# The last group's end on VectorE and ScalarE instead of accumulating transfers, and a reordered handover between two layers

## The chip, the cores and the metric

The kernel runs on one core of a Trainium2 chip. A core has TensorE (matrix products into PSUM), VectorE, ScalarE and GpSimd (elementwise work), and SyncE, whose queue issues most of the DMA transfers; ScalarE and GpSimd can issue transfers too. In the profile they are called PE, DVE, ACT, POOL and SP; SPq, ACTq and POOLq are their instruction queues. The metric is the time of one execution on the device in microseconds (us), and lower is better.

## What is computed

Two layers of attention over a graph of 4096 nodes with 512 features, all in float32. `adj` is a 4096 x 4096 matrix of edge weights, mostly zero.

```python
# layer 0
h = maximum(layernorm(x), 0)
q, k, v = h @ Wq.T + bq, h @ Wk.T + bk, h @ Wv.T + bv
x = x + softmax(q @ k.T / sqrt(512) + adj + adj) @ v
# layer 1: 8 heads of 64 features
h = maximum(layernorm(x), 0)
nX = a_ln * (X - mean) / (std + 1e-6) + b_ln        # X = h @ W, per head
kg = leaky_relu(nX @ a1 + (nX @ a2).T, 0.2) * adj    # per head, 4096 x 4096
y = softmax(where(adj != 0, kg, -32768)) @ nX + nX
out = x + elu(y)
```

The last two lines matter here. To the weighted sum of a head its own rows `nX` are added, then comes ELU, which is `maximum(y, 0) + exp(minimum(y, 0)) - 1`, and then the residual `x`, the output of layer 0.

## The kernel before

**Layer 0.** The queries are worked off in 8 chunks of 512 (`ic`), and within a chunk the keys in 32 blocks of 128 (`jt`). At the end of a chunk `chunk_end` multiplies the sums by the inverse totals and adds the rows of `x` (L810, L815), then `rows_done` updates two guards `low0` and `high0` (L824, L825). For all chunks but the last, `make_ready` spreads the work of turning the finished 512 rows into features for layer 1 over the next chunk. The features go to DRAM (`nX_d`), the own rows (`own_d`) and the rows of `x` after layer 0 (`x1_d`) too, and so do the small vectors that the scores of layer 1 are made of (`z1_d`, `z2_d`, `u4_d`, `at2m`). For the last chunk there is no next chunk; its `make_ready` runs with `last=True` inside the first steps of layer 1.

**Layer 1.** It has 512 steps, numbered n: 8 chunks of 512 queries (`ic`), 2 groups of 4 heads (`hg`), 32 blocks of 128 keys (`jt`). A step has these parts, each issued for its own n:

- `z_sums` (TensorE, L970 and L978): linear scores and masks are summed in PSUM tiles `d`. The small factors are `z1` of the group and `z2`, the masks `nb` and `nx`. The tag `d` has three buffers, and the small tiles `m` of `make_ready` and `pt1` of a group's end are taken from the same three.
- `relu` (ScalarE, L986): the upper part of the leaky ReLU for two of the four heads.
- `leaky` (VectorE, L996, L1001, L1002): the leaky ReLU for the other two heads with the broadcast rows `u4` (in the profile `u`), the product with the edge weights `g` for one head (in some steps two), and a sum for the first two.
- `weigh` (GpSimd, L1009): the product with `g` for the other three heads (or two).
- `exponent` (ScalarE, L1012), three steps later, and `values` (TensorE, L1025), four steps later, which sums into `acc`.

The edge weights and masks of four steps are loaded at a time by `load_adj` (L915 `z2`, L919 `nb`, L925 twice `nx`, L930 `g`), all on SP's queue. `open_group` loads `z1` (L943) and the two broadcasts `u4` (L946) of a group of 32 steps, ten steps ahead on SP's queue; only the first group's is called on ScalarE's queue, ahead of `load_adj(0)` in the program. `load_features` (L1109) brings the 8 blocks of features into SBUF during the first 32 steps.

**The order of the work.** Instructions marked with `seq` keep the order in which the program records them on their engine. A few others, such as the guards at the very end (L1173 to L1191), are placed by a scheduler between them. In `make_ready` a call of `at_step(d, f)` puts `f` into step 1 + d of layer 1 ahead of `leaky`; with `late=True` it comes behind `weigh`, `z_sums` and `relu` of that step. With `last=True` the statistics of the last rows, `stats` (four pairs L180 and L181 on VectorE), are called at once and thus come ahead of step 0. `deviations` (eight small operations on GpSimd, L266 to L270) and the first `norm` (ScalarE, L276) are in step 1. The transfers on SP's queue are issued in order, and each also waits for the transfer recorded eight transfers before it.

**The end of a group.** When the last `values` of a group are issued, `finish` spreads its end over the next steps, in the dictionary `later`: copies out of PSUM on ScalarE (`copies`, L1041), turning them into rows on TensorE (`to_rows`, L1047), the division (`divide`, L1056 and L1057 on VectorE), and then

- the own rows are added to `y` by an accumulating transfer that GpSimd issues (`add`, L1063),
- `minus` (L1072) and `exps` (L1076) on ScalarE make exp(minimum(y, 0)) in `e`, `positive` (L1079) makes maximum(y, 0), and `less_one` (L1082) subtracts 1,
- two more accumulating transfers (L1063) add `y` and the rows of `x1_d` to `e`,
- `close` (L1087) stores the two halves of `e` from SP's queue.

For 15 of the 16 groups this lies beside the steps of the next group. After the last group there is nothing beside it. Then the guards are reduced to one flag, which every engine loads (L73) before the kernel ends; with the given data the general path behind the flag is not entered.

Of the kernel before, what the change touches and what calls it, by code (L numbers as in the profile page):

```python
# [10 lines left out]
F32 = mybir.dt.float32  # L11
BF16 = mybir.dt.bfloat16
AF = mybir.ActivationFunctionType
ALU = mybir.AluOpType
# [4 lines left out]
P = 128  # L19
# [16 lines left out]
GC = 512  # L36
NI = N // GC
HG = 4
# [40 lines left out]
def fast_path(  # L79
# [18 lines left out]
    nc = tc.nc  # L98
    seq = tc.keep_in_program_order
# [42 lines left out]
    x1_d = dram.tile([NI, 2, P, 2, SB, P], F32, name="x1_d")  # L142
# [10 lines left out]
    own_d = dram.tile([NI, 2, P, 2, SB, P], F32, name="own_d")  # L153
# [21 lines left out]
    def means(pool, rows, name):  # L175

        st = pool.tile([P, SB, 6], F32, name=f"{name}st", tag=f"{name}st", bufs=2)
        mv = pool.tile([P, SB, 2], F32, name=f"{name}mv", tag=f"{name}mv", bufs=2)
        for b in range(SB):
            seq(nc.vector.bn_stats(st[:, b, :], rows[b]))  # L180
            seq(nc.vector.bn_aggr(mv[:, b, :], st[:, b, :]))  # L181
        return mv
# [65 lines left out]
    def make_ready(ic, x1s, small, at_step, gap, last):  # L248

        n = SB * NH  # L250
# [9 lines left out]
        def stats():  # L260
            state["mv"] = means(prep, x1s, "l")
# [164 lines left out]
            nc.sync.dma_start(out=u4_d[rows].rearrange("b h p -> (b h) p"), in_=u4c)  # L426

        if last:
            stats()
        else:  # L430
            at_step(0, stats)
        at_step(0 if last else 1, deviations)
        for b in range(SB):
            d = (0 if last else 2) + gap * b
# [28 lines left out]
    def store_rows(ic, x1s):  # L463
        for b in range(SB):
            store_block(nc.sync, x1_d, ic, b, x1s[b])


    with tc.tile_pool(name="early", bufs=2) as early, tc.tile_pool(name="kv", bufs=1) as kv:
# [70 lines left out]
        with tc.tile_pool(name="proj_c", bufs=1) as pc, tc.tile_pool(  # L539
            name="proj", bufs=2  # L540
# [96 lines left out]
            def room(first, blocks, m):  # L637
                return v[:, first : first + blocks, :].rearrange(
                    "p b d -> p (b d)"
                ).rearrange("p (m c) -> p m c", m=m)  # L640
# [37 lines left out]
            for sb in range(1, NS):  # L678
# [4 lines left out]
                if sb == 1:  # L683
                    seq(nc.sync.dma_start(
                        out=w1_sb.rearrange("p k h e -> p k (h e)"),
                        in_=w1.rearrange("(k p) o -> p k o", p=P),
# [16 lines left out]
        with tc.tile_pool(name="attn", bufs=2) as work, tc.tile_pool(  # L703
            name="attn_ps", bufs=2, space=PSUM
# [142 lines left out]
            for s in range(0, n_tiles, 2):  # L847
                ic, jt = TILES[s]
# [48 lines left out]
    with tc.tile_pool(name="ga_in", bufs=2) as inputs, tc.tile_pool(  # L897
        name="ga_g", bufs=2
    ) as adjs, tc.tile_pool(name="gat", bufs=1) as gat, tc.tile_pool(
        name="ga", bufs=2  # L900
# [3 lines left out]
        n_steps = len(STEPS)  # L904
# [30 lines left out]
        def cols(ic, hg):  # L935
            rows = slice(ic * GC, (ic + 1) * GC)
            return rows, slice(hg * HG * HD, (hg + 1) * HG * HD)

        def open_group(n, queue):

            ic, hg, _ = STEPS[n]
            z1 = inputs.tile([P, GC], BF16, name="z1", tag="z1", bufs=2)
            seq(queue.dma_start(out=z1, in_=z1_d[:, hg, ts(ic, GC)]))  # L943
            u4 = inputs.tile([P, 2, GC], F32, name="u4", tag="u4", bufs=2)
            for e in range(2):
                seq(queue.dma_start(  # L946
                    out=u4[:, e, :].rearrange("p (b i) -> p b i", i=P),
                    in_=u4_d[ic * SB : (ic + 1) * SB, hg * HG + 2 + e, :]
                    .unsqueeze(0).to_broadcast([P, SB, P]),
                ))  # L950
            groups[ic, hg] = {"z1": z1, "u4": u4}

        def pair_rows(ap, ic, hg):

            r, c = cols(ic, hg)
            return [
                ap[r, c.start + f * P : c.start + (f + 1) * P].rearrange("(b p) d -> p b d", p=P)
                for f in range(2)
            ]
# [70 lines left out]
        def finish(n, ic, hg):  # L1030

            grp = groups.pop((ic, hg))
            ob = work.tile([P, 2, GC], F32, name="ob", tag="ob", bufs=1)
            y = work.tile([P, 2, SB * 2, HD], F32, name="y", tag="y", bufs=1)

            def room():
                grp["e"] = work.tile([P, 2, SB * 2, HD], F32, name="e", tag="ob", bufs=1)

            def copies():
                for hf in range(2):  # L1040
                    seq(nc.scalar.copy(ob[:, hf, :], grp["acc"][hf]))  # L1041

            def to_rows(hf):
                pt = psum.tile([P, 2, GC], F32, name="pt1", tag="d", bufs=3)
                for b in range(SB):
                    col = (b % 2) * 2 * HB
                    seq(nc.tensor.matmul(  # L1047
                        pt[:, b // 2, col : col + 2 * HB], ob[:, hf, ts(b, P)],
                        back.rearrange("p e c -> p (e c)"), start=True, stop=True,
                    ))  # L1050
                grp["pt"] = pt[:, :, 0 : 4 * HB].rearrange("p k (q c) -> p k q c", c=HB)

            def divide(hf):
                v = grp.pop("pt")
                rinv = inverses[:, ic, hg, hf]
                seq(nc.vector.reciprocal(rinv, v[:, :, :, HD]))  # L1056
                seq(nc.vector.tensor_mul(  # L1057
                    y[:, hf].rearrange("p (k q) e -> p k q e", k=2), v[:, :, :, 0:HD],
                    rinv.unsqueeze(3).to_broadcast([P, 2, 4, HD]),
                ))  # L1060

            def add(t, what):
                seq(nc.gpsimd.dma_start(out=flat(t), in_=what, accum_op=ALU.add))  # L1063

            def of_group(ap):
                return ap[ic, hg].rearrange("p f b d -> p (f b d)")

            def flat(t):
                return t.rearrange("p f q e -> p (f q e)")

            def minus(hf):
                seq(nc.scalar.activation(grp["e"][:, hf], y[:, hf], AF.Relu, scale=-1.0))  # L1072

            def exps(hf):
                e = grp["e"][:, hf]
                seq(nc.scalar.activation(e, e, AF.Exp, scale=-1.0))  # L1076

            def positive():
                seq(nc.scalar.activation(flat(y), flat(y), AF.Relu))  # L1079

            def less_one():
                seq(nc.scalar.add(flat(grp["e"]), flat(grp["e"]), -1.0))  # L1082

            def close():
                e = grp["e"]
                for f, ap in enumerate(pair_rows(out, ic, hg)):
                    nc.sync.dma_start(  # L1087
                        out=ap, in_=e[:, f].rearrange("p (b h) e -> p b (h e)", h=2)
                    )

            for d, place, f in (
                (0, "mid", copies),
                (1, "mid", lambda: to_rows(0)), (1, "end", lambda: divide(0)),
                (2, "mid", lambda: to_rows(1)), (2, "end", lambda: divide(1)),
                (3, "end", lambda: add(y, of_group(own_d))),
                (6, "end", room), (6, "end", lambda: minus(0)), (7, "end", lambda: minus(1)),
                (8, "end", lambda: exps(0)), (8, "end", positive), (9, "end", lambda: exps(1)),
                (10, "end", less_one), (11, "end", lambda: add(grp["e"], flat(y))),
                (14, "end", lambda: add(grp["e"], of_group(x1_d))), (17, "end", close),
            ):  # L1100
                later.setdefault((n + d, place), []).append(f)

        open_group(0, nc.scalar)
        load_adj(0)

        def load_features(k):
# [15 lines left out]
        def at_step(d, f, *a, late=False):  # L1122
            (left_late if late else left).setdefault(1 + d, []).append(lambda: f(*a))
# [9 lines left out]
            for f in later.pop((n, place), []):  # L1133
                f()

        for n in range(n_steps + 22):

            q = n // JB + 1
            if n == 1:
                store_rows(NI - 1, last_rows)  # L1140
            if n % JB == (2 if q == NS - 1 else 0) and q < n_steps // JB:
                load_adj(q)
                if q < NS:
                    load_features(q)
            if n + 10 < n_steps and STEPS[n + 10][2] == 0:
                open_group(n + 10, nc.sync)
            extra(n, "top")
            if 0 <= n - 4 < n_steps:
                values(n - 4)
                if n % JB == 3:  # L1150
                    loads.pop((n - 4) // JB)
                if STEPS[n - 4][2] == NB - 1:
                    finish(n, *STEPS[n - 4][:2])
            if 0 <= n - 3 < n_steps:
                exponent(n - 3)
            extra(n, "mid")
            for f in left.pop(n, []):
                f()
            if n % JB == 2 and n // JB < NS:
                ones_in(n // JB)  # L1160
            if n < n_steps:
                leaky(n)
                weigh(n)
            if n + 1 < n_steps:
                z_sums(n + 1)
                relu(n + 1)
            for f in left_late.pop(n, []):
                f()
            extra(n, "end")
# [425 lines left out]
```

## Time and profile before

| | |
|---|---|
| time of the runs | 3947.59 us median of 3, from 3941.22 to 3955.6 |
| the profiled execution | 3945.4 us, its span 3943.6 us |
| mean TensorE clock granted | 0.987 |
| TensorE busy (PE) | 3697.2 us, 94% |
| VectorE busy (DVE) | 2869.3 us, 73% |
| GpSimd busy (POOL) | 2501.3 us, 63% |
| ScalarE busy (ACT) | 1779.9 us, 45% |

Busy shares are means over two layers with different limits. Layer 0 ends at about 2097 us; from 2400 to 2800 us, within layer 1, GpSimd is busy for 396.88 of 400 us, VectorE for 378.59, TensorE for 366.21 and ScalarE for 343.36. A line of the timeline reads: start in us from the span's start, duration in us, engine, line of the kernel, operation, output and inputs by the program's names, shapes, and in brackets how long the engine was idle before it and what ended that. Buffer numbers and trailing digits are left out of names, so `u4` stands as `u`, `x1_d` as `x_d`. For a transfer the line is its issue; when it has landed is told separately, counted from the issue.

### The profile page before, as it was taken

The numbers are of one execution on the slowest core, as the hardware profiler recorded it, in microseconds if no ns is written. First come the engines' busy times: TensorE is split into PE (matmuls) and PEld (weight loads), VectorE is DVE, ScalarE is ACT, GpSimd is POOL, SyncE is SP. The second block draws the span as 40 slices with busy tenths as digits, with TensorE's granted clock in tenths as the row PEclk, the third lists the DMA queues.
The fourth block names the chain that finished last, engine by engine and source line by source line (L and its number), as shares of the span: only waits on it lengthen the run. The fifth ranks groups of instructions, "written<-read, shape, count | busy, mean of one in ns | idle before, by whom it ended". The sixth has DMA issues, their size and how long they took to land. (4 is left out here: it accounts for less than half of the span.)

```text
span 3943.6 us, 48614 instructions
## 1 busy us (share of the span) xinstructions
PE 3697.2 (94%) x17418; PEld 1722.2 (44%) x17418; DVE 2869.3 (73%) x4299; ACT 1779.9 (45%) x1581; POOL 2501.3 (63%) x1321
## 2 busy tenths in 40 slices
PE   8989999999999999999997889999999999999996
PEld 4446666666666666666663222222222222222221
DVE  5435556565465656556566799999999999999996
ACT  1001011111111111111114688888888888888886
POOL 3432225243252524324256899999999999999996
PEclk9999999999999999999998899999999999999998
DMA  6466766768585676767567777676676777766774
GB/s 206 178 200 192 207 179 198 210 183 225 164 216 173 199 207 190 216 176 214 164 176 190 188 188 190 184 186 183 191 191 188 189 188 196 188 185 182 189 192 107
DMA packets 622778, 746.17 MB, mean 189 GB/s; under 512 B 84672, under 2 KB 467904, under 8 KB 603072
## 3 DMA queue, kind: packets, MB, share of 16 engines
q1 hardware_dynamic: 613552, 716.05, 64.3%
q0 software_dynamic: 6912, 25.17, 3.6%
q8 instruction: 138, 2.26, 0.2%
q10 hardware_dynamic: 2064, 1.77, 0.2%
q14 instruction: 112, 0.92, 0.1%
HBM read 562.23 MB, written 172.23 MB: 186 GB/s over the span
## 5 line engine op out<-in xcount | busy, mean ns | idle before, releaser
L1009 POOL TENSOR_TENSOR t<-t,g 128x1536 f32<-128x1536 f32 (+1 forms) x512 | 1704.8, 3531 | 55.7 <-DVE t L1002 48.1
L1025 PE MATMUL acc<-t,nX 128*64 128x512 f32 x4096 | 1001.7, 610 | 49.4 <-ACT t L1012 44.3
L758 POOL TENSOR_TENSOR total<-total,aT 128x512 f32<-128x512 f32 x248 | 340.1, 1371 | 1064.0 <-ACT aT L753 1055.2
L1012 ACT ACTIVATE t<-t 128x2048 f32<-128x2048 f32 x512 | 974.9, 1905 | 1.5 <-POOL t L1009 1.5
L768 PE MATMUL acc<-v,aT 128*128 128x512 f32 x2048 | 963.0, 593 | 0.0
L753 ACT ACTIVATE aT<-aT 128x512 f32<-128x512 f32 x256 | 161.2, 630 | 1323.7 <-DVE aT L748 1301.6
L986 ACT ACTIVATE t<-d 128x1024 f32<-128x1024 f32 x512 | 524.5, 1024 | 285.0 <-PE d L978 284.8
L1002 DVE TENSOR_TENSOR t<-t,d 128x1024 f32<-128x1024 f32 x512 | 619.2, 1209 | 2.8 <-ACT t L986 2.8
L768 PEld LDWEIGHTS acc<-v,aT 128*128 128x128 f32 x2048 | 390.0, 190 | 273.7 <-issue 245.6
L1025 PEld LDWEIGHTS acc<-t,nX 128*64 128x64 f32 x4096 | 251.5, 137 | 564.5 <-issue 344.7
L970 PE MATMUL d<-z,z 6*128 6x512 bf16 x2048 | 370.9, 387 | 108.2 <-DVE t L1001 59.4
L996 DVE SCALAR_TENSOR_TENSOR d<-u,at2m,d 128x512 f32<-128x512 f32 x576 | 431.7, 749 | 39.2 <-PE d L978 34.9
L748 DVE TENSOR_TENSOR aT<-aT,X 128x256 f32<-128x256 f32 x512 | 214.6, 419 | 290.0 <-PE X L740 287.0
L1001 DVE TENSOR_TENSOR t<-d,g 128x512 f32<-128x512 f32 (+1 forms) x512 | 383.9, 750 | 14.4 <-DMA g<-gT_d 7.8
L748 DVE TENSOR_TENSOR aT<-aT,Z 128x256 f32<-128x256 f32 x384 | 159.4, 415 | 306.5 <-PE Z L740 301.8
L996 DVE SCALAR_TENSOR_TENSOR t<-u,at2m,d 128x512 f32<-128x512 f32 x448 | 334.5, 747 | 46.5 <-DVE d L996 1.4
L970 PEld LDWEIGHTS <-z 6*128 6x128 bf16 x2048 | 91.9, 91 | 624.5 <-issue 404.3
L978 PE MATMUL d<-nx,ident_b 64*64 64x512 bf16 x2048 | 321.2, 392 | 1.4 <-DMA nx<-nT_d 1.2
L978 PE MATMUL d<-nb,ident_b 64*64 64x512 bf16 x2048 | 320.7, 392 | 0.0
L732 DVE SCALAR_TENSOR_TENSOR gs<-ng,aT 128x512 f32<-128x512 bf16 x256 | 279.4, 1091 | 10.2 <-DMA gT_d<-gs 1.5
L740 PE MATMUL Z<-qt,hS 128*128 128x256 f32 x1024 | 265.7, 382 | 8.3 <-DVE aT L748 8.3
L740 PE MATMUL X<-qt,hT 128*128 128x256 f32 x1024 | 264.3, 381 | 0.5 <-DVE aT L748 0.5
(171 smaller groups left out, 3154.2 us busy)
## 6 DMA issues: line engine op xcount, KB each, us to landing
g<-gT_d SPq DMA_DIRECT2D x128, 1024.0 KB, 5.5
ag<-in_adj_dram SPq DMA_DIRECT2D x256, 256.0 KB, 5.7
hT<-h_d SPq DMA_DIRECT2D x64, 1024.0 KB, 6.0
hS<-s_d SPq DMA_DIRECT2D x64, 1024.0 KB, 8.2
gT_d<-gs SPq DMA_DIRECT2D x256, 256.0 KB, 2.8
nb<-nT_d SPq DMA_DIRECT2D x128, 512.0 KB, 4.7
nx<-nT_d SPq DMA_DIRECT2D x256, 256.0 KB, 5.6
nT_d<-ng SPq DMA_DIRECT2D x256, 128.0 KB, 3.2
```

Of the source, the lines that this page charges most:

```text
L740: seq(nc.tensor.matmul(out, a, b, start=start and k == 0, stop=k == 1, skip_group_check=not start,))
L748: seq(nc.vector.tensor_add(p, p, part))
L768: seq(nc.tensor.matmul(sums[ic][b], probs[s][:, ts(b, P)], v[:, jt, :], start=jt == 0, stop=jt == NB - 1))
L970: seq(nc.tensor.matmul(pair[hh // 2][:, hh % 2, :], z2[rows, ts(jt % JB, P)], groups[ic, hg]["z1"][rows, :], start=True, stop=False,))
L978: seq(nc.tensor.matmul(pair[hh // 2][ts(c, HD), hh % 2, :], ident_b[rows, rows], masks[r != c][rows, jt % JB, :], start=False, stop=True,))
L986: seq(nc.scalar.activation(t[:, 0:2, :], zs[n][0], AF.Relu, scale=4.0))
L996: seq(nc.vector.scalar_tensor_tensor(pair[1][:, e, :] if e > 1 - mine else t[:, 2, :], u4[:, e, :], at2m[:, jt, h : h + 1], pair[1][:, e, ...
L1001: seq(nc.vector.tensor_mul(t[:, HG - mine : HG, :], pair[1][:, 2 - mine : 2, :], g))
L1002: seq(nc.vector.tensor_add(t[:, 0:2, :], t[:, 0:2, :], pair[0]))
L1009: seq(nc.gpsimd.tensor_mul(t[:, 0:mine, :], t[:, 0:mine, :], g))
L1012: seq(nc.scalar.activation(logits[n], logits[n], AF.Exp))
L1025: seq(nc.tensor.matmul(grp["acc"][hf][ts(e, HD), :], nX[jt // SB][:, jt % SB, hg * HG + 2 * hf + e, :], t[:, 2 * hf + e, :], start=jt == 0 ...
```

## The change

It has three parts.

1. In layer 1's first steps the statistics of the last rows are no longer recorded ahead of step 0. They are put at the end of step 0, behind its `leaky` and `weigh` and behind `z_sums` and `relu` of step 1.
2. The first group's `z1` and `u4` are issued on SP's queue. As `open_group(0)` stands ahead of `load_adj(0)`, they now come first in that queue.
3. The last group's end is a straight sequence of its own. Own rows and rows of `x1_d` are loaded by two ordinary transfers into a tile of the tag `t` when the last step has been recorded. The additions are VectorE operations on halves of 128 x 512; ScalarE makes exp(minimum(y, 0)) as before; the maximum, and the sum with the -1 in it, are VectorE's. The two halves are stored from SP's and from ScalarE's queue. The loop is shortened to match.

```diff
         if last:
-            stats()
+            at_step(-1, stats, late=True)
         else:
             at_step(0, stats)
...
+            if n > n_steps:
+
+                of_rows = [last_in[0][:, 2 * k : 2 * k + 2, :] for k in range(2)]
+
+                def half(t, hf):
+                    return t[:, hf].rearrange("p q e -> p (q e)")
+
+                copies()
+                to_rows(0)
+                divide(0)
+                to_rows(1)
+                divide(1)
+                room()
+                e = grp["e"]
+                for hf in range(2):
+                    seq(nc.vector.tensor_add(half(y, hf), half(y, hf), of_rows[0][:, hf]))
+                    minus(hf)
+                    exps(hf)
+                    seq(nc.vector.tensor_scalar_max(half(y, hf), half(y, hf), 0.0))
+                for hf, queue in enumerate((nc.sync, nc.scalar)):
+                    seq(nc.vector.scalar_tensor_tensor(
+                        half(e, hf), half(e, hf), -1.0, half(y, hf), ALU.add, ALU.add
+                    ))
+                    seq(nc.vector.tensor_add(half(e, hf), half(e, hf), of_rows[1][:, hf]))
+                    queue.dma_start(
+                        out=pair_rows(out, ic, hg)[hf],
+                        in_=e[:, hf].rearrange("p (b h) e -> p b (h e)", h=2),
+                    )
+                return
...
-        open_group(0, nc.scalar)
+        open_group(0, nc.sync)
         load_adj(0)
...
-        for n in range(n_steps + 22):
+        last_in = []
+        for n in range(n_steps + 4):
 
             q = n // JB + 1
+            if n == n_steps:
+
+                last_in.append(work.tile([P, HG, GC], F32, name="t", tag="t", bufs=6))
+                for k, ap in enumerate((own_d, x1_d)):
+                    seq(nc.sync.dma_start(
+                        out=last_in[0][:, 2 * k : 2 * k + 2, :].rearrange("p f c -> p (f c)"),
+                        in_=ap[NI - 1, 1].rearrange("p f b d -> p (f b d)"),
+                    ))
```

## The prediction

> **What bounds the kernel now.** I read the page first, then the chain of waits, then the timeline of the two places that the diff touches. The page:
>
> ```profile
> span 3943.6 us, 48614 instructions
> PE 3697.2 (94%) x17418; PEld 1722.2 (44%) x17418; DVE 2869.3 (73%) x4299; ACT 1779.9 (45%) x1581; POOL 2501.3 (63%) x1321
> L1009 POOL TENSOR_TENSOR t<-t,g 128x1536 f32<-128x1536 f32 (+1 forms) x512 | 1704.8, 3531 | 55.7 <-DVE t L1002 48.1
> ```
>
> Layer 0 (to 2097 us) is TensorE's. In layer 1 VectorE and GpSimd feed each other, 95% and 99% busy (378.6 and 396.9 of 400 us from 2400): a step's `weigh` costs GpSimd 3.5 us. The change leaves TensorE's instructions in the same order, and GpSimd's too but for three accumulating DMAs at the end, so the 1800 us between the two places have no reason to change. What counts is when layer 1 starts and what lies behind its last step. There the chain of waits (start, duration, what) consists of time in which the engine waited for nothing but a transfer:
>
> ```profile
> 3908.66 7.17 issue
> 3915.96 10.40 issue
> 3927.25 4.24 issue
> ```
>
> The end, in the timeline (start, duration, engine, line; in brackets the idle time and its releaser):
>
> ```profile
> 3910.65 1.94 PE L1025 MATMUL acc<-t,nX 128*64 128x512 f32 x8 [0.59 <-ACT t L1012]
> 3914.85 0.69 DVE L1057 TENSOR_TENSOR y<-pt,inverses 128x512 f32<-128x512 f32 x1
> 3915.84 0.89 POOL L1063 DMA_DIRECT2D y<-own_d  x1 [7.19 <-DVE y L1057]
> 3921.86 1.15 ACT L1072 ACTIVATE e<-y 128x512 f32<-128x512 f32 x2 [8.63 <-DMA y<-own_d]
> 3925.02 1.06 ACT L1082 ACTIVATE e<-e 128x1024 f32<-128x1024 f32 x1
> 3926.38 0.87 POOL L1063 DMA_DIRECT2D e<-y  x1 [9.64 <-ACT e L1082]
> 3931.50 0.87 POOL L1063 DMA_DIRECT2D e<-x_d  x1 [4.25 <-DMA e<-y]
> 3936.98 0.93 SPq L1087 DMA_DIRECT2D out_dram<-e  x2
> ```
>
> After the last division (ends 3915.54) every stage waits for a transfer: own rows 6.0 us from issue, ELU on ScalarE 4.2, then two more additions by DMA, 5.1 and 5.5 us from start to the next start. 21.4 us in a row, nothing beside it.
>
> The handover, also in the timeline:
>
> ```profile
> 2085.53 0.33 SPq L915 DMA_DIRECT2D z<-z_d  x1
> 2086.66 1.18 ACTq L946 DMA_DIRECT2D u<-u_d  x2
> 2087.72 0.60 SPq L930 DMA_DIRECT2D g<-gT_d  x1
> 2098.44 1.02 ACT L986 ACTIVATE t<-d 128x1024 f32<-128x1024 f32 x1 [11.76 <-PE d L978]
> 2100.20 0.18 DVE L181 BATCH_NORM_AGGREGATE lmv<-lst 128x2 f32<-128x6 f32 x1
> 2102.27 0.75 DVE L996 SCALAR_TENSOR_TENSOR d<-u,at2m,d 128x512 f32<-128x512 f32 x1 [1.89 <-DMA u<-u_d]
> 2105.67 3.45 POOL L1009 TENSOR_TENSOR t<-t,g 128x1536 f32<-128x1536 f32 x1 [17.59 <-DVE t L1002]
> 2114.07 1.22 DVE L1002 TENSOR_TENSOR t<-t,d 128x1024 f32<-128x1024 f32 x1 [2.80 <-ACT t L986]
> ```
>
> VectorE does the last rows' statistics (2097.10 to 2100.38), then waits 1.89 us for the broadcasts `u4`. The landing answers say 15.0 us for the second broadcast (2087.1 to 2102.1) and 14.0 us for `g`:
>
> ```profile
> DMA to landing us min/median/max: 9.5/12.2/15.0
> DMA to landing us min/median/max: 14.0/14.0/14.0
> ```
>
> `g` lands at 2087.7 + 14.0 = 2101.7, only 0.4 us before `u4`. It is wanted next (L1001 at 2103.7).
>
> **What the skill says.** The Trainium skill, "DMA: Bandwidth & Descriptors", section "Queues, rings and completion order": each DMA engine consumes one queue's descriptors in ring order and takes turns between queues by packets. The trace agrees: later on, with broadcasts ahead on SP's queue, the `nb` load issued at 2334.7 lands after 10.6 us, against 3.9 us for that of 2318.3 without them. The same page, "Anatomy of one DMA — SWDGE (gpsimd) path", gives 2.0 us plus bytes over 436 GB/s, an estimate of 3.2 us for 512 KB; here the accumulating ones take 4.8 to 5.9, so I use the trace. "VectorE: DVE Perf Modes", section "Walkthrough: the 8-slice pipeline in each mode": a float32 tensor_scalar out of SBUF can run two elements per cycle, a tensor_tensor only one; L730 (0.42) and L1001 (0.68 us) agree.
>
> **The end, step by step.** The start is the same, 3915.54. Removed: three accumulating DMAs with their 6.0 + 5.1 + 5.5 us, the two whole-tile passes on ScalarE. Added on VectorE per half of 128x512: two additions (0.68 each, as L1001; an SBUF-only one was not seen, between 0.55, 512 elements at one per cycle, and 0.7), one maximum (0.42 as L730; 0.3 to 0.7), one scalar_tensor_tensor (0.75, as L996). That is 2 x 2.53 = 5.06. The flag's instructions (0.41, 0.41, 0.14, 0.14, 0.28, 0.15, 0.14) are interleaved with them by the built order, 1.6 us. ScalarE: 0.58 + 0.61 per half. In order: first addition to 3916.2; two reductions and a small one to 3917.05; ScalarE's negative part is done by 3916.85, so the maximum goes at once, to 3917.45; second addition 3918.15; ScalarE 3918.25 to 3918.85 and exp to 3919.45; VectorE waits for TensorE's small transpose until 3918.7, worst 3919.0, maximum 3919.4, then 0.75 + 0.15 + 0.68: first half at 3921.0; flag at 3921.9; second half at 3922.55. The last issue starts near 3922.65 on ScalarE's queue, against 3937.45 (the second of the two at 3936.98): 14.8 us earlier. Behind it the kernel takes about the same (here 5.7 us from the end of the issue to the end of the span: landing 2.3, flag load and branch). As the first half goes out 1.6 us earlier on SP, nothing is added there; for five engines branching together I allow 0.3. **End: 14.5 us**, from 13 to 15.5.
>
> What hides the two new loads (512 KB each, on SP at step 512): their `t` slot is free when the values of step 506 are done, near 3900.2; a 1 MB `g` takes 5.5 us (median), so they are there near 3907, 8 us before the first addition. Nothing is queued behind them but the output. Without that cover, the addition would wait as long as they are late.
>
> **The handover.** SP issues `z1` and both broadcasts first, from 2085.5: 0.34 + 1.18 = 1.5 us, and z2, `nb`, `nx`, `g` each go out 1.5 us later. ScalarE loses three issues; it idles there anyway (11.76 us). The broadcasts, now first in an idle queue at 2085.9 and 2086.5, land after 6.9 to 11.5 us (30 on SP's queue), by 2098.0 at the latest. Then the masks decide: `d` is ready for VectorE at 2098.3 now. What is late next is `g`. The bytes before it are the same 2.8 MB, so if the engines only swap the order it lands where it did, 2101.7. In the steady case above it landed 10.6 us after the second broadcast (2342.1 to 2352.7); 2094.0 + 10.6 gives 2104.6. I take 2103. The first two VectorE operations are then done, and the first step ends at 2103.0 + 0.15 + 0.6 + 1.21 = 2105.0 against 2105.54: 0.5 us won; at the ends `g` by 2099.8 wins 3.9, `g` at 2106.5 loses 3.
>
> The statistics (3.28 us) now stand between steps 0 and 1. Queued behind them is step 1 on VectorE, and `weigh(1)` for it. But GpSimd first does `weigh(0)` (3.45) and the deviations (3.08), and VectorE idles 2.80 in step 2, waiting for ScalarE behind the `norm` that waits for these deviations. Statistics end 3.3 us after step 0, GpSimd wants them 3.55 after it: covered, with 0.25 to spare. Step 1 ends 6.75 after step 0, where `weigh(1)` started 6.7 after it. Cost 0.2; if the cover fails, 0.5 (3.28 - 2.80). **Handover: +0.3**, from -3 to +3.9. Later the step rhythm is unchanged, so this shift reaches the end.
>
> **Sum.** 14.5 + 0.3 = 14.8. Of the profiled execution (3945.4 us, span 3943.6): 3930.6. The median 3947.59 is 2.2 higher: 3932.8. I say 3932, 0.4% less.
>
> **Rivals.**
> 1. The broadcasts no longer matter and `g` comes early: step 0 starts at 2098.3, ends at 2101.6, 3.9 won, 3928. For it: transfer engines were only half busy from 2090 to 2093. Against: the same half-busy stretch follows broadcasts at 2336 to 2338.
> 2. The masks and `g` queue up behind the broadcasts more than counted: `g` at 2106 to 2107, handover 2 to 3 us lost, 3935. For it: 10.6 against 3.9 us for `nb`.
> 3. Slower: the broadcasts, alone at the head of SP's queue, hold up everything behind them. Its place is `g`'s landing. If they took until 2102.1 as now and the rest only then its 10.6 us, `g` lands at 2112.7 and 10 us go: no change. The gain of the end is eaten from a landing of about 2118; with broadcasts of twice 15.0 us it is 2127, and the time 3956. Against it: 11.5 us is the longest of the 30 on SP's queue, with 1.5 MB ahead.
> 4. The end doesn't shrink fully: own rows land late, or the closing 5.7 us grow, since all engines now load the flag at once behind an output in flight. 6 us less gain, 3938. Against: engines that load the flag early took 0.5 to 1.6 us.
>
> **Numbers.** The forecast 0.64, first rival 0.12, second 0.14, third 0.04, fourth 0.06. A measurement of this kernel tells 0.3% (11.8 us) from no change; three runs of before spread over 14 us, so a median is uncertain by some 5. The likeliest case alone spans 3925 to 3940 with that; with rivals 1, 2 and half of 4, 3922 to 3943. Faster by over 0.3%: nearly all of rival 1, most of the forecast (a gain of 14.8 minus noise), a third of 2: 0.72. Slower 0.05, same 0.23.
>
> **What would show it.** In the changed profile: no GpSimd DMA at the end; last output issue 7 us after the last division (was 22); from there 5 to 6 us to the end. At the handover: L996 starts at about 2098.3 without waiting for `u4`, and L1001 waits for `g` to about 2103; `weigh(0)` near 2105; statistics behind it. Wrong if `weigh(0)` starts after 2107, if step 2 ends more than 10.5 us after step 0, or if the first addition waits for its rows.

## The result

The changed kernel takes 3937.22 us (median of 19 runs, 3930.75 to 3942.38); the kernel before, run beside it, 3943.81 (19 runs, 3938.52 to 3955.6). The ratio is 0.9983, 95% interval 0.9976 to 0.9989: 6.7 us faster (4.3 to 9.5). That is clear of zero, but within the 0.3% that were to count as no change. The forecast was 3932, a gain of 14.8. Its time is within the range; its gain is more than twice the measured one.

The page of the kernel after:

```profile
span 3931.9 us, 48617 instructions
PE 3693.1 (94%) x17418; PEld 1719.4 (44%) x17418; DVE 2873.8 (73%) x4307; ACT 1778.2 (45%) x1579; POOL 2498.0 (64%) x1318
```

Busy shares are as before, so the two places have to be read in the timeline. First the end:

```profile
3916.88 0.69 DVE L1057 TENSOR_TENSOR y<-pt,inverses 128x512 f32<-128x512 f32 x1
3917.49 0.68 DVE L1106 TENSOR_TENSOR y<-y,t 128x512 f32<-128x512 f32 x1
3918.94 0.43 DVE L1109 TENSOR_SCALAR y<-y 128x512 f32<-128x512 f32 x1
3922.49 0.39 SPq L1115 DMA_DIRECT2D out_dram<-e  x1
3923.06 0.69 DVE L1114 TENSOR_TENSOR e<-e,t 128x512 f32<-128x512 f32 x1
3923.83 0.41 ACTq L1115 DMA_DIRECT2D out_dram<-e  x1
```

No transfer stands in the chain any more: the first addition (L1106) follows the division at once, and the last issue starts 6.26 us after the last division ends (3917.57), against 21.91 before.

The handover, where the surprise is:

```profile
2083.52 0.98 SPq L946 DMA_DIRECT2D u<-u_d  x2
2085.58 3.17 SPq L925 DMA_DIRECT2D nx<-nT_d  x2
2088.79 1.02 SPq L930 DMA_DIRECT2D g<-gT_d  x1
2090.88 2.88 SPq L1138 DMA_DIRECT2D nX<-nX_d  x4
2099.72 0.76 DVE L996 SCALAR_TENSOR_TENSOR d<-u,at2m,d 128x512 f32<-128x512 f32 x1 [4.48 <-PE d L978]
2106.13 0.69 DVE L1001 TENSOR_TENSOR t<-d,g 128x512 f32<-128x512 f32 x1 [4.87 <-DMA g<-gT_d]
2108.08 3.43 POOL L1009 TENSOR_TENSOR t<-t,g 128x1536 f32<-128x1536 f32 x1 [22.37 <-DMA nX<-nX_d]
2128.73 0.69 DVE L309 COPY x<-m 128x512 f32<-128x512 f32 x1 [6.79 <-DMA x_d<-x]
```

VectorE doesn't wait for `u4` any more, but waits 4.87 us for `g`. And a second wait has appeared, 6.79 us behind stores of `x1_d`. (The bracket of L1009 names features, which landed at the same moment. `weigh(0)` starts 0.13 us after the end of L1002, as it did before.)

```profile
DMA to landing us min/median/max: 17.3/17.3/17.3
```

This is `g` from its issue at 2088.8: 17.3 us, where it was 14.0. It lands at 2106.1. It was also issued late, 5.6 us after the first transfer of the handover (L943) and not 2.2 us after it (L915) as before: the two issues of `nx` ahead of it took 3.17 us, 2.49 of them the second. Before, the two took 1.30:

```profile
2086.37 1.30 SPq L925 DMA_DIRECT2D nx<-nT_d  x2
```

The end of layer 0 moves by some microseconds from execution to execution, so the table counts from the start of the last product group of layer 0 (L806). "Step 0" is the start of the sum L1002 in step 0, "step 4" the same in step 4; "rest" is the time from the last division to the end of the span. Besides the first profiles it has a second one of before, after, and the handover alone. All in us.

| kernel | L806 at | step 0 | step 4 | last division ends | rest |
|---|---|---|---|---|---|
| before | 2093.06 | 11.27 | 31.78 | 1822.48 | 28.06 |
| before, again | 2090.56 | 10.76 | 31.35 | 1820.96 | 28.28 |
| after | 2090.68 | 16.06 | 40.78 | 1826.89 | 14.33 |
| after, again | 2094.31 | 16.35 | 41.08 | 1834.64 | 14.35 |
| end only | 2093.18 | 12.41 | 33.33 | 1823.74 | 14.58 |
| handover only | 2089.98 | 15.56 | 37.32 | 1825.45 | 27.87 |
| handover only, again | 2098.69 | 14.68 | 39.50 | 1827.28 | 28.43 |
| end and statistics | 2092.79 | 10.02 | 31.35 | 1822.02 | 14.09 |
| features behind `g` | 2098.35 | 11.83 | 33.84 | 1825.61 | 14.24 |
| stores first | 2093.32 | 15.49 | 36.65 | 1826.18 | 14.30 |
| broadcasts in layer 0, ahead of `hT` | 2105.46 | 7.69 | 29.57 | 1818.12 | 14.02 |
| broadcasts in layer 0, behind `hT` | 2091.96 | 7.79 | 29.52 | 1821.16 | 14.38 |
| broadcasts last | 2093.88 | 9.68 | 31.01 | 1823.31 | 13.71 |
| the same, one output queue | 2092.31 | 8.35 | 29.78 | 1819.67 | 13.92 |

The four profiles with the changed handover against the two of before, by their means: step 0 15.7 against 11.0 (4.6 lost), step 4 39.7 against 31.6 (8.1 lost), last division 1828.6 against 1821.7 (6.8 lost). In the two with the new end the rest gains 13.8.

### The profile page after: what moved, and what is told of

It is laid out like the page before. It is cut to its first block, busy times and chain, and to the rows that moved or that the text cites. A ratio compares the mean times of both kernels' runs of the same rounds, so it can differ in the third digit from the quotient of the medians.

```text
span 3931.9 us, 48617 instructions
## 1 busy us (share of the span) xinstructions
PE 3693.1 (94%) x17418; PEld 1719.4 (44%) x17418; DVE 2873.8 (73%) x4307; ACT 1778.2 (45%) x1579; POOL 2498.0 (64%) x1318
## 5 line engine op out<-in xcount | busy, mean ns | idle before, releaser
L1009 POOL TENSOR_TENSOR t<-t,g 128x1536 f32<-128x1536 f32 (+1 forms) x512 | 1705.9, 3579 | 60.8 <-DVE t L1002 29.9
L1002 DVE TENSOR_TENSOR t<-t,d 128x1024 f32<-128x1024 f32 x512 | 619.2, 1209 | 0.1
L996 DVE SCALAR_TENSOR_TENSOR d<-u,at2m,d 128x512 f32<-128x512 f32 x576 | 431.7, 750 | 40.7 <-PE d L978 38.2
L1001 DVE TENSOR_TENSOR t<-d,g 128x512 f32<-128x512 f32 (+1 forms) x512 | 384.0, 750 | 15.5 <-DMA g<-gT_d 8.9
L996 DVE SCALAR_TENSOR_TENSOR t<-u,at2m,d 128x512 f32<-128x512 f32 x448 | 334.6, 747 | 46.5 <-DVE d L996 1.4
L732 DVE SCALAR_TENSOR_TENSOR gs<-ng,aT 128x512 f32<-128x512 bf16 x256 | 279.4, 1091 | 10.3 <-DMA gT_d<-gs 1.7
```

Source lines behind the costliest of these rows:

```text
L996: seq(nc.vector.scalar_tensor_tensor(pair[1][:, e, :] if e > 1 - mine else t[:, 2, :], u4[:, e, :], at2m[:, jt, h : h + 1], pair[1][:, e, ...
L1001: seq(nc.vector.tensor_mul(t[:, HG - mine : HG, :], pair[1][:, 2 - mine : 2, :], g))
L1002: seq(nc.vector.tensor_add(t[:, 0:2, :], t[:, 0:2, :], pair[0]))
L1009: seq(nc.gpsimd.tensor_mul(t[:, 0:mine, :], t[:, 0:mine, :], g))
```

## The experiments

**The end alone.** The handover is put back, the new end stays:

```diff
-            at_step(-1, stats, late=True)
+            stats()
-        open_group(0, nc.sync)
+        open_group(0, nc.scalar)
```

> Only the new end; statistics and the first broadcasts as in the kernel before. All theories: the end is worth 13 to 14 us wherever the handover stands, so the time is 3930 (ratio 0.9965), and the way from the last product of layer 0 (TensorE, L806) to the last VectorE operation of step 0 (L1002) stays 11.3 us, to that of step 4 31.8 us. If the end is worth only the 6.6 us that the whole change brought, 3937.

Measured: 3932.78 us (6 runs), ratio 0.9964 (0.995 to 0.9977), 14.2 us of gain. The end brings what the forecast gave it, and the whole change brings less than this part of it.

**The handover alone.** The old end, the new handover (the two edits above the other way round, in the kernel before).

> The handover of the changed kernel with the old end. Theory A (the handover loses what the trace of the changed kernel shows, whatever the end is): counted from the last product group of layer 0, step 0 adds at about 16 us, step 4 at about 41 us, the last division ends 3 to 5 us later than in the kernel before, the end stays at 28 us, so the ratio to the kernel before is about 1.001 (3 to 5 us slower). Theory B (the steps of the prediction were right about the handover and the 16 us belong to one execution): step 0 within 0.5 us of the kernel before, ratio 1.000, no loss over 1 us.

Measured: 3950.59 us (19 runs) against 3943.92, ratio 1.0019 (1.0012 to 1.0026): 7.5 us slower (4.7 to 10.3). The two parts add up: 14.2 - 7.5 = 6.7. With a gain of the end known to 9 to 20 us only, that the sum fits to the tenth is chance. Theory A holds in kind, but its loss of 3 to 5 us was too small, and step 4 is at 37.32 and not 41. In this first profile the last division is only 3.0 us later, less than the timed runs say; hence the second profiles.

**Three second profiles.** Kernels as named; each is one execution.

> The kernel before, profiled once more, to see how far two executions of one kernel scatter. If one profiled execution can be trusted to 1.5 us counted from the last product group of layer 0: step 0 at 10 to 12.5 us (it was 11.27), the last division at 1821 to 1824 us (it was 1822.48), while that product group itself may stand anywhere from 2090 to 2098 us. If instead the loss at the handover is scatter, step 0 can be at 14 us or later here too.

> The changed kernel, profiled once more. If the loss at the handover is its own: step 0 at 15 to 17 us again, g landing 16 to 18 us after its issue, the last division at 1825 to 1828 us, the rest 14.3 us. The second loss at step 4 may be there or not, since the same handover with the old end showed it at 37.3 us instead of 40.8. If the first profile was an outlier: step 0 at 13 us or earlier.

> The handover alone, profiled once more. Its timed runs say 5 to 10 us slower, its first profile only 2.8 us when counted from the last product group of layer 0. If the first profile caught a lucky execution: the last division at 1827 us or later and the time some 5 us or more above the second profile of the kernel before. If some of the loss sits in front of that product group: it stands later than in the kernel before by the missing 2 to 4 us. If neither: again about 1825.5 us, and the missing part stays within the scatter of the medians.

Measured (table): before again at 10.76, so the loss at step 0 is no scatter. After again at 16.35, `g` landing after 17.8 us, but its last division at 1834.64, outside what was expected; the handover again at 1827.28. A last division can thus differ by 7.8 us between two executions of one kernel, and single profiles can't price a loss of this size. The means above (6.8) and the timed runs (7.5) agree within this scatter.

**The statistics with the end, broadcasts as before.** Of the changed kernel only the queue is put back:

```diff
-        open_group(0, nc.sync)
+        open_group(0, nc.scalar)
```

> The changed kernel with the first broadcasts back on ScalarE's queue: end and statistics as changed. If the broadcasts at the head of SP's queue are the cause of the late handover (theory 1 or 2): step 0's L1002 9.4 to 11.3 us after L806 (16.1 in the changed kernel), step 4's at about 31 (40.8), time 3928 to 3930. If the moved statistics are the cause (theory 3): step 4 still at 36 or more, time 3935 and above.

Measured: 3931.16 us (6 runs), ratio 0.9964 (0.9952 to 0.9976), as the end alone. Step 0 at 10.02, step 4 at 31.35. Moving the statistics costs nothing and wins nothing that can be told; the loss comes from the place of `z1` and the two broadcasts. (It is the broadcasts: the runs below that leave only `z1` first on SP's queue don't lose at step 0.)

**Features behind `g`.** In the changed kernel a transfer of 64 bytes out of `g` stands ahead of `load_features(0)` on SP's queue, so that features and second loads go out only when `g` is there:

```diff
+        landed_d = dram.tile([1, 16], F32, name="landed_d")
+        seq(nc.sync.dma_start(out=landed_d, in_=loads[0][0][0:1, 0, 0:16]))
         load_features(0)
```

> The changed kernel with one tiny transfer added on SP's queue that reads the edge weights g of the first steps, so that the features and the loads for step 4 are issued only when g has landed. Theory 1 (the broadcasts themselves, ahead in the ring, hold up g): g still lands 16 us or more after its issue, step 0's L1002 at about 16 after L806, and the time is the same or longer than 3937. Theory 2 (SP gets to the features too early and they share the engines with g): g lands at most 13 us after issue, step 0's L1002 at 12 or less.

Measured: 3935.82 us (6 runs), ratio 0.997 (0.9958 to 0.9982). The time alone doesn't tell the theories apart, the landing does. `g`, issued at 2096.8 here:

```profile
DMA to landing us min/median/max: 12.8/12.8/12.8
```

17.3 became 12.8, and step 0 stands at 11.83 instead of 16.06. So 4.5 us of `g`'s landing come from transfers issued behind it. This is one execution; in the five profiles with features close behind `g` and the broadcasts first it took 16.0 to 17.8.

**Broadcasts last.** In the changed kernel `load_adj(0)` stands between `z1` and the broadcasts; SP's queue carries masks, `g`, then `u4`:

```diff
             u4 = inputs.tile([P, 2, GC], F32, name="u4", tag="u4", bufs=2)
+            if n == 0:
+                load_adj(0)
             for e in range(2):
```

(the call behind `open_group(0, nc.sync)` goes).

> The changed kernel with the two broadcasts behind masks and g on SyncE's queue. Theory A (what stands ahead on one queue lands first, and whatever is last is late): masks land after 4 to 8 us and g after about 12 us, but now the broadcasts land after 13 us or more and VectorE's first operation waits for them: step 0 at 12 to 15 us, between the kernel before and the changed one. Theory B (only the features and the second set of loads, which SyncE now issues early, slow everything down): g still lands after 16 us or more and step 0 stands at 15 us or later.

Measured: 3931.75 us (5 runs), ratio 0.9963 (0.9949 to 0.9977). `g`, issued at 2089.0, and the broadcasts, issued at 2089.7 and 2090.2:

```profile
DMA to landing us min/median/max: 8.1/8.1/8.1
...
DMA to landing us min/median/max: 9.8/10.5/11.2
```

```profile
2101.51 0.76 DVE L998 SCALAR_TENSOR_TENSOR d<-u,at2m,d 128x512 f32<-128x512 f32 x1 [3.06 <-DMA u<-u_d]
```

`g` lands after 8.1 us, and the last of all these loads, a broadcast, 15.1 us after the first issue (2086.35 to 2101.4). In the changed kernel the same bytes take 23.0 us (2083.15 to 2106.1). The expectation had `g` after about 12 and step 0 at 12 to 15; step 0 is at 9.68, earlier than in the kernel before. So the order on the one queue makes the loss, not the queue. Landings from their issue, in us; the two columns after `g` count from the first transfer of the handover, which is issued 7.53 us ahead of L806 in each of these kernels:

| order | `u4` | `nb` | `nx` | `g` | `g` issued | `g` there | features from |
|---|---|---|---|---|---|---|---|
| before (`u4` on ScalarE's queue) | 9.5, 15.0 | 4.2 | 7.1, 9.1 | 14.0 | 2.2 | 16.2 | 5.5 us behind `g` |
| after | 7.6, 8.7 | 11.0 | 12.0, 12.8 | 17.3 | 5.6 | 23.0 | 2.1 us behind `g` |
| features behind `g` | 5.8, 8.7 | 10.5 | 11.8, 11.9 | 12.8 | 6.0 | 18.7 | `g`'s landing |
| broadcasts last | 9.8, 11.2 | 3.3 | 5.6, 6.0 | 8.1 | 2.7 | 10.7 | 5.1 us behind `g` |

Of the 9.2 us between 17.3 and 8.1, 4.5 lie with what comes behind `g`, 4.7 with the broadcasts ahead of it. But they also hold up the issue: in all six profiles with the broadcasts first the second issue of `nx` took 1.9 to 3.3 us, in the eight others 0.6. Counted to where `g` is there, the broadcasts' place is worth 8.0 us (18.7 to 10.7), what comes behind 4.2. What holds the issue is not shown.

What the engines did meanwhile, in stretches of 4 us (per stretch its length, then busy time and instructions of PE, PEld, DVE, ACT, POOL, then PE's clock, the DMA engines' busy share, GB/s), after:

```profile
2087.00:2091.00 4.00, 4.00 (x13) 1.85 (x12) 0.00 (x0) 0.00 (x0) 0.00 (x0) 1.00 0.99 175
2091.00:2095.00 4.00, 0.67 (x10) 0.62 (x9) 3.21 (x9) 0.00 (x0) 0.00 (x0) 0.93 1.12 205
2099.00:2103.00 4.00, 1.55 (x7) 0.24 (x6) 1.50 (x2) 1.02 (x1) 0.00 (x0) 0.50 1.10 163
```

and with the broadcasts last:

```profile
2087.00:2091.00 4.00, 4.00 (x11) 1.83 (x10) 0.00 (x0) 0.50 (x1) 1.26 (x1) 1.00 0.83 238
2091.00:2095.00 4.00, 3.83 (x16) 2.07 (x14) 0.13 (x1) 0.00 (x0) 0.00 (x0) 1.00 1.05 259
2095.00:2099.00 4.00, 0.84 (x8) 0.33 (x12) 3.32 (x11) 0.00 (x0) 0.00 (x0) 0.81 1.01 271
```

The engines count as busy or nearly so in both, but move 163 to 205 GB/s in the one and 238 to 271 in the other (200 from 2099 to 2103, when features go out there too). So the busy share doesn't tell what is moved. In the first two stretches of the changed kernel the broadcasts are under way until 2092.7, so it fits that they occupy the engines with few bytes while the loads wait. In the third they have long landed, and `g` shares the engines with features. How the loss divides within the engines was not tested.

**Stores first.** The second wait: the copy of the features (L309) writes rows whose `x1_d` stores have to be out, and these now stand behind the second set of loads.

```diff
-            if n == 1:
+            if n == 0:
                 store_rows(NI - 1, last_rows)
```

> The changed kernel, with the stores of the last rows ahead of the second set of loads on SyncE's queue instead of behind it. Theory A (the second loss, between steps 3 and 4, is the copy of the features waiting for these stores): the idle time of 6.8 us ahead of that copy falls under 1 us, step 4 stands at 34 to 37 us instead of 40.8, and, since half of such a shift reached the end, the last division ends about 2 us earlier: about 3935 us. Theory B (it only follows from g being late, or the stores now share the engines with g and make it later still): step 0 later than 17 us, step 4 again at 40 us or more, 3937 us or more.

Measured: 3935.02 us (12 runs), ratio 0.9975 (0.9966 to 0.9983). The wait is gone, only TensorE is waited for:

```profile
2127.18 0.69 DVE L309 COPY x<-m 128x512 f32<-128x512 f32 x1 [3.15 <-PE m L303]
```

Step 4 is at 36.65 instead of 40.78, as theory A had it. What it is worth at the end is not resolved: the intervals of the two ratios (0.9966 to 0.9983 and 0.9976 to 0.9989) overlap.

**Broadcasts in layer 0.** The two broadcasts are loaded in the last chunk of layer 0 into tiles that are free there, and copied by ScalarE at the handover:

```diff
+                if jt == 22 and ic == NI - 1:
+                    load_first_group()
...
+                if n == 0:
+                    seq(nc.scalar.copy(u4[:, e, :], first_u4[e]))
+                    continue
```

> The changed kernel, but the first group's two broadcasts are loaded into two free tiles during the last chunk of layer 0 and copied into place by ScalarE (2 x 0.6 us) at the handover; z1 stays first on SP's queue. Theory 1: with the broadcasts gone from the handover g lands 2 to 4 us earlier than in the kernel before, step 0's L1002 7.5 to 9 us after L806, step 4's at 28 to 30, time 3926 to 3928. Theory 2: the features still come early and take g's share, step 0's L1002 at 11 or more, time 3930 and above.

Measured: 3939.12 us (21 runs), ratio 0.998 (0.9973 to 0.9987). The expected time was missed. The handover does win (step 0 at 7.69), but L806 stands at 2105.46. The timeline shows the place, a product of the last chunk that waits for the hidden rows `hT`:

```profile
2067.92 2.07 PE L741 MATMUL Z<-qt,hT 128*128 128x256 f32 x4 [9.27 <-DMA hT<-h_d]
```

In the kernel before this wait is 2.82 us. The broadcasts went out at 2055.34, just ahead of the load of these rows at 2056.56. (This execution was already some 5 us late before that, so of the late L806 only about 6 can be laid on the wait.) To see if that is the cause, they go out behind it:

```diff
-                if jt == 22 and ic == NI - 1:
+                if jt == 26 and ic == NI - 1:
```

> As the run with the broadcasts loaded in layer 0, but behind the last load of hidden rows instead of ahead of it. Theory A (that run lost in layer 0 what it won at the handover, because the broadcasts went out just ahead of the hidden rows): the idle time behind the hidden rows falls from 9.3 us to about 4 us, the last group of layer 0 starts near 2093 us instead of 2105 us, step 0 stays at about 8 us and the last division at about 1818 us from there, the end at 14 us, so about 3927 us (ratio 0.9955): faster than both kernels. Theory B (the late layer 0 was that execution's own, the handover's gain is lost again in the groups after it): the time stays near 3937 us, or the last division is at 1822 us or later.

Measured: 3928.76 us (5 runs), ratio 0.9956 (0.9943 to 0.997). L806 is at 2091.96 again, step 0 at 7.79. The same wait, in the timeline of this kernel:

```profile
2056.45 1.13 PE L741 MATMUL Z<-qt,hT 128*128 128x256 f32 x4 [3.04 <-DMA hT<-h_d]
```

Theory A holds, in the wait and in the timed runs, whose interval lies clear of that of the run before it (0.9973 to 0.9987). The last division is at 1821.16 and not 1818: of the 3.2 us that step 0 won against the two profiles of before 0.6 are left there, which one execution can't tell from scatter.

**One queue for the output.** The stretch from the end of the last issue to the end of the span grew from 5.7 to 7.7 us. In the kernel with the broadcasts last:

```diff
-                for hf, queue in enumerate((nc.sync, nc.scalar)):
+                for hf, queue in enumerate((nc.sync, nc.sync)):
```

> The kernel with the broadcasts last, with both halves of the last output on SyncE's queue instead of one on each of SyncE's and ScalarE's. Theory A (the stretch from the last issue to the end grew from 5.7 to 7.7 us because the half on ScalarE's queue takes 4.2 us to land and those on SyncE's 2.3 to 2.8): the second half lands within 3 us, the stretch is 5.8 to 6.3 us, the part from the last division to the end 12 to 12.6 us instead of 13.7 to 14.4. Theory B (it grew because the engines now come to the last branch together, or because the two halves are nearer each other than the loads before): the half lands after 4 us again or the stretch is 7 us or more. The time in both cases within 3 us of the kernel with the broadcasts last, about 3930 us.

Measured: 3927.68 us (5 runs), ratio 0.9958 (0.9944 to 0.9971). Landing of the two output transfers, first after, then with one queue:

```profile
DMA to landing us min/median/max: 2.3/3.2/4.2
```

```profile
DMA to landing us min/median/max: 2.3/3.3/4.2
```

Theory A falls: the second half takes 4.2 us on SP's queue too; the stretch is 7.3. The old end had 2.3 and 2.8, with issues 0.5 us apart and not 1.3. Why the second is slower is open. In the traces, while it is under way (3924.4 to 3928.0 in the changed kernel) the DMA engines also carry six packets of the queues that the profile calls instruction, 0.06 MB, with one output queue too; while the two old halves were under way they carried one. Whether these hold it up was not tested.

Five kernels beat the kernel before and, by intervals that hardly touch, the change as it was made: the end alone, the end with the statistics, and the three that keep broadcasts out of the way of `g` (last on the queue, with one or two output queues, or in layer 0 behind the hidden rows). The intervals of the five overlap, so no best one is named.

## Why the prediction was right and wrong

- **What bounds the kernel: right.** The middle was left alone, and what the experiments can tell apart comes from the handover and the end. The 1800 us between scatter by up to 7.8 us from execution to execution.
- **The end, 14.5 us: right in mechanism and sum, two terms off.** Measured 14.2 by time, 13.8 by the profiles. Last issue after last division: 7.1 computed, 6.26 measured, since VectorE's operations were added up at their full duration and overlap a little: the first addition is 0.68 us long, and the next starts 0.60 after it. The seven flag instructions add to 1.67 and not 1.6. The lines that the prices were taken from are of other forms (L1001 reads `d` out of PSUM, L730 writes bf16), but the prices held: the new additions, float32 in SBUF, took 0.68, the maxima 0.43 and 0.40, and the sums with -1 0.67 and 0.68 instead of 0.75. "Behind it the kernel takes about the same", 5.7 plus 0.3, measured 7.7: 1.4 of this is the landing of the second half (4.2 against 2.8). That is the fourth rival in small, 1.7 us beyond the allowance where it named 6. The new loads were hidden: issued at 3902.26 and 3902.65, they were there at 3907.2, 10 us before the first addition.
- **"`u4` no longer waited for": right; `d` ready at 2098.3: 3.8 us off.** L996 waits for TensorE's `d` now and starts at 2099.72, which is 2102.1 on the clock of the kernel before (L806 was 2.4 us earlier here). The masks already carry part of the queueing.
- **"If the engines only swap the order it lands where it did": the step that failed.** I took 2103 for `g`; it landed at 2106.1, or 2108.5 on the clock of the kernel before. The working counted bytes ahead of `g` and took their order for neutral. (Its 2.8 MB include the 1 MB of `g` itself, and before, the second broadcast landed 0.5 us after `g`, so it was not all ahead of it.) Of the 5.5 us that it came later than 2103, 1.9 are its issue: all loads were to go out 1.5 us later, `g` went out 3.4 us later. The other 3.5 are the landing, 17.3 us where 2103 allowed 13.8. The runs show what stands behind both: the broadcasts ahead of it cost 4.7 us of landing and 3.3 of issue against the run that has them last, the features and second loads that SP issued behind it 4.5 of landing. The late issue could have been read beforehand: behind the broadcasts of a later group, at 2335.20, the two issues of `nx` took 2.73 us. So could the transfers behind it, since a transfer on SP's queue waits for the one recorded eight before it, and the features stand eight behind the broadcasts. Before, the second broadcast lands at 2102.2 and the last two features go out when it is there, in the timeline of before:

```profile
2093.25 9.72 SPq L1109 DMA_DIRECT2D nX<-nX_d  x4
2103.02 1.36 SPq L915 DMA_DIRECT2D z<-z_d  x1
```

  After, the broadcasts land by 2092.7, the features are issued by 2093.76, and the second loads begin at 2096.09. The late broadcasts had kept traffic away from `g`. The steady-state value of 10.6 us that the choice leaned on has no features behind `g`, and the next loads only 4.1 us behind it (2344.76).
- **The skill's ring order: right as far as it goes.** The section "Queues, rings and completion order" of the Trainium skill's page "DMA: Bandwidth & Descriptors" says that an engine takes one queue's descriptors in ring order. The order of landings agrees (`u4`, `nb`, `nx`, `g` in order of issue). It doesn't make an order free: `nb` behind the broadcasts needs 11.0 us, ahead of them 3.3.
- **The statistics' cover: right.** From step 0 to step 3 it takes 14.0 us in both kernels (25.28 - 11.27 and 30.05 - 16.06); a cost of 0.2 was computed.
- **"This shift reaches the end": about right on average, not in one execution.** 4.6 us at step 0 are 6.8 at the last division, with the wait for the stores between, which no step of the prediction had: I counted transfers moved past `g`, but not the stores behind the second loads. What this wait costs at the end is not resolved.
- **Handover +0.3, from -3 to +3.9: measured -7.5 by time, -4.6 at step 0.** Both lie outside the range. The second rival named the mechanism (masks and `g` behind the broadcasts, `g` at 2106 to 2107) and a loss of 2 to 3 us, but not the transfers behind `g`. The third rival's slower total didn't come: `g` at 2108.5 is far from the 2118 that it needed. By the prediction's own test, "wrong if `weigh(0)` starts after 2107", the handover's part is wrong: it started at 2108.08. The two other tests held: step 2 ends 9.8 us after step 0, and the first addition doesn't wait.
- **The time** is within the range in part by luck. The end was priced right, and the range of some 20 us is wider than the miss of the handover. But the gain was taken 8.1 us too large and the base 3.8 us too high: its three runs lay that much over the median of the 19 that ran beside the changed kernel. The two errors partly cancel, so that 3932 is only 5.2 us off. A gain over 0.3% had been given 0.72, no change 0.23; no change is what came.

## What to carry to other kernels

Put loads on a queue in the order of need, and price a moved load by what it delays on that queue and by what it releases behind it: a slot that comes free early lets later loads start, and they share the engines with the one that is waited for. In this kernel the broadcast loads belonged behind the big load or far ahead of it, and not just ahead of any load that was due. When a change has two parts, measure each: here one part won 14 us, the other gave half of it back, and the sum looked like nothing.

## What was not expected of the hardware

- The order of the same loads on one queue changed the time for all of them from 15.1 to 23.0 us (in the latter with more of the next loads among them), with the DMA engines counted as busy or nearly so in both.
- With two broadcast loads first on the queue, the issue of a later 256 KB load took 1.9 to 3.3 us instead of 0.6. Not explained.
- The second of two output transfers of 256 KB landed after 4.2 us when issued 1.3 us behind the first, on either queue, and after 2.8 when issued 0.5 us behind it. Not explained; six instruction packets were moved beside the former, one beside the latter.
- Two executions of one kernel, at clocks of 0.990 and 0.988, differed by 7.8 us in the 1830 us of layer 1, so that a single profile could not price a loss of 7 us.
